# A 16-column bf16 product for one half of the array ahead of a stretch of unmasked attention scores

## The chip, the cores and the metric

The kernel runs on one core of a Trainium2 chip. The metric is the device time of one execution in microseconds, the median of three runs. Besides, one execution was taken by the hardware profiler; every row of a profile below is of that one execution.

## The reference

The model is two layers over eight batches of 512 tokens with 256 channels: a layer norm and attention (causal attention over the tokens plus cross attention to a context of 512 rows), a feed-forward block with quantised weights and activations, then cross attention to the same context and a second quantised feed-forward block. The change touches the attention scores of all three attentions, with 16 heads of 16 channels each:

```python
att  = jnp.einsum('bhqd,bhkd->bhqk', q, k) * scale
att  = jnp.where(causal[None, None], att, -jnp.inf)      # "S": causal
y    = jnp.einsum('bhqk,bhkd->bhqd', jax.nn.softmax(att, axis=-1), v)
attc = jnp.einsum('bhqd,bhkd->bhqk', qc, kc) * scale     # "C": to the context, no mask
y    = y + jnp.einsum('bhqk,bhkd->bhqd', jax.nn.softmax(attc, axis=-1), vc)
...
scores = jnp.einsum('bhqd,bhkd->bhqk', qh, kh) * scale   # "X": second layer, no mask
```

## The kernel before, in words

The attention work is cut into 24 units: eight causal ones (S), eight of the first layer's cross attention (C) and eight of the second layer's (X). A unit has four groups of four heads, and a group's scores are computed twice. First they are computed with queries on the partitions, into a pair of PSUM banks, only to find each row's maximum (`max_one`, L668; in the profile `pair<-qk`, read by VectorE as `mx<-pair`). Later they are computed with keys on the partitions, the maximum already subtracted through two extra rows, into two single banks, and ScalarE takes the exponential (`exp_one`, L756; in the profile `bank<-qk`, read by ScalarE as `p<-bank`). The exponentials are then multiplied with the values (`av_part`, `bank<-p,v`).

One call of `max_one` or `exp_one` is called a visit here. A visit handles two heads at once: head c=0 lies on partitions 0 to 63 and head c=1 on partitions 64 to 127, so that two products with a contraction over at most 64 rows use the two halves of the TensorE array side by side. In a C or X unit a visit is two f32 matmuls of 512 columns, one for each half, each with its own load of 128 weight columns. There are 8 max visits and 8 exp visits in a group, so 32 and 32 in a unit, and 512 and 512 in the 16 units of kind C and X.

In an S unit a visit begins with the mask: `masks` (L646) issues two small bf16 products (k = 0, 1) for each half that write minus 1e30 above the diagonal, and the f32 scores then add to them. In a C or X unit nothing stands ahead of the scores, and the first of them starts the bank anew (`start=off == 0 and kind != "S"`).

The order of all instructions on TensorE is fixed when the kernel is built. `Plan` holds clocks for the engines and estimates for each operation; the loop at L1452 picks, step by step, a max visit, an exp visit, a product with the values or a piece of another job (projections, transposes, feed-forward), and `plan.pe` moves TensorE's clock. The plan knows two ways of using the array that concern us: "rows" (two halves of 64 rows, all visits) and "cols" (four strips of 32 output columns, nearly all else), with a price for going from one to the other (`SWITCH`). So TensorE's stream is an alternation of stretches: some matmuls in columns, then one or several visits in a row, then columns again. A visit that follows matmuls of another kind is called a head below; one that follows another visit is called chained.

Which semaphores a visit waits for: the first matmul that writes a bank waits until VectorE (for a pair) or ScalarE (for a single bank) has read what stood there; `Writer.matmul` (L258) adds these waits to the first writer of a bank.

Of the kernel before, what the change touches and what calls it, by code (L numbers as in the profile page):

```python
# [76 lines left out]
class Plan:  # L77
# [39 lines left out]
    def op(self, kind, n, *deps):  # L117
        fixed, rate = RATE[kind]
        return self.run(kind.rstrip("2"), fixed + n * rate, *deps)
# [105 lines left out]
GQ, AHEAD = 4, 3  # L225
LINGER = 0.2
ROW_COLS = 600
DVE_HANDICAP = 0.8


# [56 lines left out]
def build(tc, A, out):  # L287
    nc = Engines(tc)
# [8 lines left out]
    plan = Plan()  # L297
# [3 lines left out]
    def tile(tag, shape, dtype, name, pool=wp):  # L301
        return pool.tile(shape, dtype, tag=tag, name=name, bufs=BUFS[tag])
# [52 lines left out]
    ident2 = const.tile([P, 2, P], BF16, name="ident2")  # L355
    mask2 = const.tile([P, 2, P], BF16, name="mask2")
# [29 lines left out]
    def evacuate(dst, src, n, *deps, bias=None):  # L386

        if plan.would("act", n, *deps) <= plan.would("dve", n, *deps) + DVE_HANDICAP:
            if bias is None:
# [256 lines left out]
    def masks(ps, c, blocks, keys):  # L646

        diag = ps.rearrange("p (a b) -> p a b", b=P)[:, blocks]  # L650
        rows = slice(64 * c, 64 * c + 64)
        for k in range(2):
            lhs, rhs = (mask2, ident2) if keys else (ident2, mask2)
            cols = slice(64 * k, 64 * k + 64 if keys else P)
            n = len(range(*blocks.indices(NT)))
            nc.tensor.matmul(
                diag[:, :, cols], lhs[rows, k], rhs[rows, k, cols].unsqueeze(1).broadcast_to([64, n, cols.stop - cols.start]),
                start=k == 0, stop=False, skip_group_check=True,
            )

    def max_ready(s):
        G, i = MAX_STEPS[s]
        t = plan.bank_at("sm")
        if ("stack", G) not in at or t is None or (i == 0 and G % 2 == 0 and not plan.rings["mx"]):
            return None
        return max(at["stack", G], t)

    def max_one(s):  # L668

        G, i = MAX_STEPS[s]  # L670
        kind, _ = UNITS[G // 4]
        p, qts = MAXS[kind][i]
        n = G // 2
        if i == 0 and G % 2 == 0:
            heapq.heappop(plan.rings["mx"])
            mx_t[n] = tile("mx", [P, 2, 4, NT], F32, f"mx{n}")
        pb = plan.bank_take("sm")
        ps = pairs[pb // 2]
        pair = 2 * (G % 2) + p
        size = [(qt + 1) * P if kind == "S" else T for qt in qts]  # L680
        offs = [sum(size[:x]) for x in range(len(qts))]
        if kind == "S":

            first = size[0] // P - 1
            step = size[-1] // P
            for c in range(2):
                masks(ps[:, c], c, slice(first, first + (len(qts) - 1) * step + 1, step), False)
            plan.pe(len(qts) * 192 + 60, mode="rows")
        for off, w, qt in zip(offs, size, qts):
            for c in range(2):  # L690
                q, k = (qk_t[n % NQK][64 * c : 64 * c + 48, pair, x] for x in range(2))
                nc.tensor.matmul(
                    ps[:, c, off : off + w], q[:, qt * P : (qt + 1) * P], k[:, :w],
                    start=off == 0 and kind != "S", stop=True, skip_group_check=True,
                )
        t = plan.pe(sum(size), mode="rows")
        for off, w, qt in zip(offs, size, qts):
            nc.vector.tensor_reduce(
                mx_t[n][:, :, pair, qt], ps[:, :, off : off + w], AX.X, ALU.max, negate=True
            )  # L700
            t = op("dve", 2 * w, t)
        plan.bank_give("sm", pb, t)
        if s + 1 == len(MAX_STEPS) or MAX_STEPS[s + 1][0] != G:
            at["max", G] = t

    def rows_job(n):
# [16 lines left out]
        for qt in range(NT):  # L723
            for h, i in enumerate(got):
# [4 lines left out]
                )  # L729
        tm = plan.pe(ROW_COLS, "rows")  # L730
        t = 0.0
# [24 lines left out]
    def exp_one(s):  # L756


        G, i = EXP_STEPS[s]
        kind, _ = UNITS[G // 4]  # L760
        p, kts = EXPS[kind][i]
        n = G // 2
        pair = 2 * (G % 2) + p
        pb = plan.bank_take("st", 2)
        tp, slots = zip(*(heapq.heappop(plan.p_free) for _ in range(2)))
        pt = [wp.tile([P, T], F32, tag=f"p{slots[c]}", name=f"p{G}_{i}_{c}", bufs=1) for c in range(2)]
        ps, off = [banks[x] for x in pb], 0
        if kind == "S":
            step = (T - kts[0] * P) // P
            for c in range(2):  # L770
                masks(ps[c], c, slice(0, (len(kts) - 1) * step + 1, step), True)
            plan.pe(len(kts) * P + 80, mode="rows")
        for kt in kts:
            q0 = kt * P if kind == "S" else 0
            w = T - q0
            for c in range(2):
                q, k = (qk_t[n % NQK][64 * c : 64 * c + 50, pair, x] for x in range(2))
                nc.tensor.matmul(
                    ps[c][:, off : off + w], k[:, kt * P : (kt + 1) * P], q[:, q0:],
                    start=off == 0 and kind != "S", stop=True, skip_group_check=True,  # L780
                )
                p_t[G, kt, 2 * p + c] = pt[c][:, off : off + w]
            off += w
        t = plan.pe(off, mode="rows")
        if s + 1 == len(EXP_STEPS) or EXP_STEPS[s + 1][0] != G:
            at["exp", G] = t
        tm = t
        for c in range(2):
            nc.scalar.activation(pt[c][:, :off], ps[c][:, :off], AF.Exp, scale=0.25)
            t = op("act", off, tm, tp[c])  # L790
            plan.bank_give("st", pb[c], t, c == 1)
        for kt in kts:
            p_at[G, kt, p] = t
        p_slots[G, kts[-1], p] = slots
# [657 lines left out]
    while plan.jobs or a < len(AV_STEPS):  # L1452
        ready = {
            "a": av_ready(a) if a < len(AV_STEPS) else None,
            "e": exp_ready(e) if e < len(EXP_STEPS) else None,
            "m": max_ready(m) if m < len(MAX_STEPS) else None,
        }
        can = {k: t is not None and t + LAT <= plan.now for k, t in ready.items()}
# [18 lines left out]
        if any(can.values()):  # L1477
            k = min(urgent)[1] if urgent else "e" if closing and can["e"] else "a" if can["a"] else min((feed[k], k) for k in "me" if can[k])[1]
            if k == "a":
                av_part(a)  # L1480
                a += 1
            elif k == "m":
                max_one(m)
                m += 1
            else:
                exp_one(e)
                e += 1
            idle = 0
        else:
            times = [t + LAT for t in ready.values() if t is not None] + [max(j[0], plan.now) for j in plan.jobs]  # L1490
            plan.clock["pe"] = max(before + 1e-3, min(times, default=before))
            idle += 1
            assert idle < 20000, (m, e, a)
# [100 lines left out]
    for bs in ((0,), (1,), (2, 3), (4, 5), (6, 7)):  # L1594
# [3 lines left out]
        for f in range(8):  # L1598
            i = 8 * b + n * f
            ps = [banks[2 + i % 6]] if n == 1 else [pairs[1 + f % 3][:, x] for x in range(2)]  # L1600
# [29 lines left out]
    def bias_first(i):  # L1630
        ps = half_banks[i % 8]
        nc.tensor.matmul(ps, ones3, b2p.rearrange("p t c -> p (t c)"), start=True, stop=False, skip_group_check=True)
        return ps.rearrange("p (t c) -> p t c", t=2)
# [53 lines left out]
    for i in range(2 * NB):  # L1687
# [4 lines left out]
        ps = half_ps.pop(i, None)  # L1692
        if ps is None:
            ps = bias_first(i)
# [79 lines left out]
```

## Time and profile before

| what | value |
|---|---|
| median of three runs | 1464.75 us (1461.56 to 1465.69) |
| the profiled execution, its own time | 1460.25 us |
| its span, first to last instruction | 1458.4 us |
| TensorE (PE) busy | 1374.8 us, 94%, 14400 matmuls and as many weight loads |
| VectorE (DVE) busy | 1142.0 us, 78% |
| ScalarE (ACT) busy | 1035.5 us, 71% |
| GpSimd (POOL) busy | 681.6 us, 47% |
| mean granted TensorE clock | 0.971 |

PE is the matmul side of TensorE, PEld its weight loads, which can overlap with matmuls. In the timeline a row gives the start, the length, the engine, the line, what is written and read, and how many instructions were merged; the end of a matmul is modelled, so that distances are best taken from start to start. A row such as `50*128 50x512 f32` is a product over 50 rows with 128 weight columns and 512 streamed columns.

### The profile page before, as it was taken

To read this page: it belongs to the slowest core of one execution; us is meant where nothing else is said; L and a number is where in the kernel's file an instruction comes from. 1 tells how busy PE (TensorE), PEld (TensorE's weight loads), DVE (VectorE), ACT (ScalarE), POOL (GpSimd) and SP (SyncE) were. 2 spreads that over 40 slices of the span, in tenths; PEclk is the share of its full clock that TensorE was granted. 3 is DMA by queue.
4 is the path that set the end of the run, shared out by engine and by line. 5 is a ranking of instruction groups with operands and counts; after the bars stand their busy time and mean duration, and the time that the engine had idled before them with its cause. 6 is when DMAs were issued, how large, how long until landed. Compare 5 with 4: busy or idle time off the path is not lost. (4 is left out here: it accounts for less than half of the span.)

```text
span 1458.4 us, 36089 instructions
## 1 busy us (share of the span) xinstructions
PE 1374.8 (94%) x14400; PEld 597.5 (41%) x14400; DVE 1142.0 (78%) x1591; ACT 1035.5 (71%) x1904; POOL 681.6 (47%) x1025
## 2 busy tenths in 40 slices
PE   4999999999999999999999999999999998999978
PEld 2443444444444444434344433443333333333527
DVE  4678588697788886898777996689899888766397
ACT  1456767677768867767677777668778795777587
POOL 1463355465455465464653552654455541524332
PEclk8899999999999999999899999999999999999899
DMA  6593565667576755665457655556647657373343
GB/s 126 152 216 76 133 139 125 142 138 182 132 161 150 161 129 141 156 161 126 105 126 155 163 126 132 142 120 160 163 105 169 155 149 196 105 176 110 117 142 116
DMA packets 155612, 207.03 MB, mean 142 GB/s; under 512 B 71940, under 2 KB 74244, under 8 KB 154932
## 3 DMA queue, kind: packets, MB, share of 16 engines
q1 hardware_dynamic: 155444, 204.73, 58.0%
q8 instruction: 113, 1.85, 0.5%
q14 instruction: 55, 0.45, 0.1%
HBM read 68.15 MB, written 47.43 MB: 79 GB/s over the span
## 5 line engine op out<-in xcount | busy, mean ns | idle before, releaser
L241 DVE TENSOR_REDUCE mx<-pair 128x2 f32<-128x1024 f32 (+3 forms) x768 | 808.9, 1086 | 210.7 <-PE pair L259 194.6
L241 ACT ACTIVATE p<-bank 128x512 f32<-128x512 f32 (+1 forms) x1408 | 712.0, 587 | 232.7 <-PE bank L259 224.8
L259 PE MATMUL bank<-p,v 128*32 128x512 f32 (+3 forms) x3072 | 371.7, 563 | 2.9 <-DVE mrow L241 1.3
L259 PE MATMUL bank<-qk 50*128 50x512 f32 (+3 forms) x1536 | 337.6, 433 | 16.2 <-ACT p L241 8.0
L259 PE MATMUL pair<-qk 48*128 48x512 f32 (+3 forms) x1536 | 325.5, 438 | 25.7 <-DVE mx L241 11.8
L259 PEld LDWEIGHTS bank<-qk 50*128 50x128 f32 x1536 | 159.6, 190 | 215.7 <-ACT p L241 142.9
L259 PEld LDWEIGHTS pair<-qk 48*128 48x128 f32 x1536 | 148.0, 191 | 171.5 <-DVE mx L241 83.4
L384 POOL TENSOR_SCALAR qkt<-qkt 128x512 fp32r<-128x512 f32 x92 | 57.1, 621 | 164.1 <-ACT qkt L241 157.5
L241 ACT ACTIVATE qkt<-bank,qk_bias 128x512 f32<-128x512 f32 x96 | 66.6, 693 | 81.0 <-PE bank L259 65.4
L409 POOL TENSOR_TENSOR qkt<-qkt 128x512 fp32r<-128x512 f32 x92 | 118.8, 1291 | 7.7
L259 PEld LDWEIGHTS bank<-p,v 128*32 128x32 f32 x3072 | 70.9, 109 | 114.6 <-issue 85.9
L384 POOL TENSOR_SCALAR mhl<-mx 128x32 fp32r<-128x32 f32 x48 | 11.8, 245 | 171.3 <-DVE mx L241 164.8
L883 POOL TENSOR_TENSOR yt<-oc,rb 128x512 f32<-128x512 f32 x31 | 39.8, 1283 | 73.3 <-DMA rb<-scrz 50.9
L259 PE MATMUL pair<-mask,ident 64*128 64x128 bf16 (+2 forms) x768 | 58.0, 226 | 6.9 <-DVE mx L241 4.7
L259 PE MATMUL bank<-ident,mask 64*128 64x64 bf16 (+1 forms) x768 | 52.7, 206 | 3.7 <-ACT p L241 1.2
L259 PEld LDWEIGHTS <-ident 64*128 64x128 bf16 x768 | 26.1, 97 | 71.0 <-issue 52.8
L259 PEld LDWEIGHTS <-mask 64*128 64x128 bf16 x768 | 25.8, 96 | 69.3 <-issue 61.0
L241 ACT COPY v<-bank 128x512 f32<-128x512 f32 x44 | 26.2, 596 | 39.4 <-PE bank L259 39.1
L241 ACT COPY ev<-bank 128x512 f32<-128x512 f32 x56 | 33.5, 598 | 17.9 <-PE bank L259 17.9
L241 DVE SCALAR_TENSOR_TENSOR h<-bank,so,bc_l_b 128x512 f32<-128x512 f32 x64 | 45.3, 741 | 0.9 <-PE bank L259 0.7
L241 ACT ACT_TABLE_LOAD x34 | 43.6, 1283 | 1.9 <-PEq L1762 0.7
L1189 POOL TENSOR_SCALAR h<-h,sh 128x1024 f32<-128x1024 f32 x32 | 36.0, 1125 | 17.7 <-DVE sh L241 15.2
(230 smaller groups left out, 1686.4 us busy)
## 6 DMA issues: line engine op xcount, KB each, us to landing
qk<-qkt SPq DMA_DIRECT2D x288, 256.0 KB
scro<-ev SPq DMA_DIRECT2D x94, 256.0 KB
oc<-scro SPq DMA_DIRECT2D x47, 256.0 KB
rb<-scrz SPq DMA_DIRECT2D x47, 256.0 KB
x_d<-xb SPq DMA_DIRECT2D x15, 512.0 KB
xa_s<-in_x SPq DMA_DIRECT2D x8, 512.0 KB
xb<-in_x SPq DMA_DIRECT2D x8, 512.0 KB
xr<-x_d SPq DMA_DIRECT2D x16, 256.0 KB
```

Of the source, the lines that this page charges most:

```text
L241: r = f(*args, **kw)
L259: r = self.eng.matmul(out, *args, **kw)
L384: nc.gpsimd.tensor_scalar(dst, src, 1.0, 0.0, ALU.mult, ALU.add)
L409: nc.gpsimd.tensor_tensor(dst, full, high.bitcast(F32), ALU.subtract)
L883: nc.gpsimd.tensor_tensor(y, o, rb, ALU.mult)
L1189: nc.gpsimd.tensor_scalar(ht, ht, s[:, t - t0 : t - t0 + 1], MAGIC, ALU.mult, ALU.add)
```

## The change

A new helper, `first_of_visit`, issues one bf16 matmul: its weights are `ident2[:64, 0]` (64 rows, 128 columns), the streamed operand is 16 columns of the mask (`NFIRST`), and the result goes to the first 16 columns of the c=0 half's score tile. Both visits call it in C and X units, at the place where an S visit has its masks, but it issues only if the plan's mode is not yet "rows": at a head, not in a chained visit. The scores that follow start the bank anew, so what it wrote is overwritten. Being the first writer of its bank, it takes over the wait for that bank. The plan's clock and mode are not moved by it, so the order of everything else stays.

```diff
+NFIRST = 16
...
+    def first_of_visit(ps):
+        if plan.mode != "rows":
+            nc.tensor.matmul(
+                ps[0][:, :NFIRST], ident2[:64, 0], mask2[:64, 0, :NFIRST], start=True, stop=True, skip_group_check=True
+            )
...
             plan.pe(len(qts) * 192 + 60, mode="rows")
+        else:
+            first_of_visit([ps[:, c] for c in range(2)])
         for off, w, qt in zip(offs, size, qts):
...
             plan.pe(len(kts) * P + 80, mode="rows")
+        else:
+            first_of_visit(ps)
         for kt in kts:
```

## The prediction

> **What bounds the kernel now.** I read the page first, then the groups by shape, then the timeline of TensorE in places where it did not wait, then the waits and the clock.
>
> ```profile
> PE 1374.8 (94%) x14400; PEld 597.5 (41%) x14400; DVE 1142.0 (78%) x1591; ACT 1035.5 (71%) x1904; POOL 681.6 (47%) x1025
> PE   4999999999999999999999999999999998999978
> PEclk8899999999999999999899999999999999999899
> ```
>
> TensorE is the busiest engine in nearly every slice; its matmuls are what the end waits for, though not at every moment:
>
> ```profile
> DVE mx L241 <- PE pair L259: 194.6, 239, 8.1
> PEld bank L259 <- ACT p L241: 157.8, 250, 2.6
> ```
>
> VectorE waited 194.6 us for max scores, and weight loads for exp scores waited 157.8 us for ScalarE to free a bank (part of that under running matmuls). So the engines take turns in holding each other up, and time added on TensorE counts in full only where it leads.
>
> The change adds a bf16 weight load and a 16-column matmul at the head of a stretch of visits. What a head costs now:
>
> ```profile
> L259 PEld LDWEIGHTS bank<-qk 50*128 50x128 f32 x1536 | 159.6, 190 | 215.7 <-ACT p L241 142.9 <-issue 34.4 <-DVE mx L241 10.0
> L259 PEld LDWEIGHTS <-mask 64*128 64x128 bf16 x768 | 25.8, 96 | 69.3 <-issue 61.0 <-DVE mx L241 3.0 <-DVE h L241 0.8
> ```
>
> An f32 load of scores lasts 190 ns, a bf16 load of the mask products 96. Next, TensorE's matmuls, start to start:
>
> ```profile
> 211.71 0.49 PE L259 MATMUL bank<-qk 50*128 50x512 f32 x2
> 212.14 0.42 PE L259 MATMUL bank<-p,v 128*32 128x128 f32 x8
> 212.49 0.49 PE L259 MATMUL bank<-qk 50*128 50x512 f32 x2
> 212.82 0.39 PE L259 MATMUL pair<-qk 48*128 48x512 f32 x2
> 213.15 0.64 PE L259 MATMUL bank<-xlt_s,w_Cq 128*32 128x512 f32 x4
> ```
>
> A lone visit (211.71 to 212.14) takes 0.43 us, 0.424 in the trace's finest numbers; a stretch of two (212.49 to 213.15) takes 0.66. The second visit costs only 0.23, because its weights came early:
>
> ```profile
> 1065.55 0.50 PE L259 MATMUL bank<-qk 50*128 50x512 f32 x2
> 1065.65 0.19 PEld L259 LDWEIGHTS pair<-qk 48*128 48x128 f32 x2
> 1065.88 0.40 PE L259 MATMUL pair<-qk 48*128 48x512 f32 x2
> 1066.21 0.64 PE L259 MATMUL bank<-p,v 128*32 128x512 f32 x4
> ```
>
> The second visit's load (1065.65) starts 0.23 us ahead of its matmul, under the first visit. The first visit's load has nothing to hide under: 0.10 us of each head is weights. A masked head has the change's pattern, bf16 ahead of f32:
>
> ```profile
> 68.16 0.24 PE L259 MATMUL bank<-ident,mask 64*128 64x64 bf16 x4
> 68.23 0.48 PE L259 MATMUL bank<-qk 50*128 50x512 f32 x2
> 68.64 0.27 PE L259 MATMUL bank<-l0w1s,one 128*128 128x1 f32 x1
> 68.16 0.12 PEld L259 LDWEIGHTS <-mask 64*128 64x128 bf16 x4 [0.20 <-issue]
> 68.20 0.20 PEld L259 LDWEIGHTS bank<-qk 50*128 50x128 f32 x2
> ```
>
> It takes 0.476 us to the next kind of work (68.16 to 68.64). The f32 load starts at 68.20 and the stretch ends 0.435 us after that; in the lone visit above it ends 0.424 after its load. Other masked heads agree (0.427 where a 64x128 mask stands ahead). So one rule covers heads: the end comes 0.425 to 0.435 us after the f32 weight load starts, whatever ran before it.
>
> **The change part by part.** It removes no work and moves none. It adds one load and one matmul per head. Chained visits get nothing, since the helper issues only when the mode is not "rows". Counted through the trace, 406 of the 1024 unmasked visits follow a matmul of another kind (222 exp, 184 max); 13 more follow the max rows' small transposes, where the mode is "rows" already. So 406 loads and 406 matmuls; TensorE goes from 14400 to 14806. No DMA, no VectorE, ScalarE or GpSimd instruction is added, and no queue is passed.
>
> Cost at one head: how much later does the f32 load of half c=0 start? In the masked heads, the second bf16 load starts 15 ns after the first one of the same half: a second weight set goes in as soon as the first product has its own. At a head of the changed kernel the f32 load is the second in that place, so it starts about 15 ns later than now; the end after it comes 0 to 10 ns later than the lone visit's (0.425 to 0.435 against 0.424). That gives 15 to 25 ns; I take 20. Streaming 16 columns (64 took 29 ns from the second mask product to the scores) runs under the f32 load. The c=1 half's load is not held up, but its matmul is issued behind that of c=0.
>
> Bounds: from above the masked exp head, which costs 0.476 - 0.424 = 52 ns with two bf16 products of 64 columns for each half; one product of 16 for one half can't well cost more. From below zero: the f32 load still has to come after the start of the stretch, and masked heads do not start sooner after the column work before them (0.525 us from its last matmul, 0.522 unmasked), so I see no gain at a head. Nearest row: 20 ns.
>
> The added instruction takes over the bank wait, so behind it stand the f32 load and all of TensorE's queue, as they stood behind the f32 load before; no wait is new. Where the head had waited, VectorE or ScalarE had just freed the bank and the 20 ns come after that.
>
> One rule of the Trainium skill speaks against the change: "TensorE: Matmul & The Clock Gate", Part 3 (The mechanism), says that a weight load runs beside matmuls in flight only if its row group differs. The f32 load of c=0 has the same rows as the small product, so it would wait for it, about 0.19 us (the shortest mask matmul), and 406 x 0.19 = 77 us would be lost. The trace disagrees: at 68.20 the f32 load runs while mask products of the same rows last to 68.40, and the load of 1065.65 runs under a matmul of the same rows. (Part 2 of the page, step 1, does allow a load into a background weight buffer ahead of matmuls in flight; that fits.) I follow the trace.
>
> Sum: 406 x 20 ns = 8.1 us on TensorE. How much reaches the end? Followed back from the last exp matmul, going at each wait to what ended it, TensorE holds 785 of 1347 us, and 213 of the 406 heads lie on that path: 213 x 20 ns = 4.3 us if the path stays. With more work TensorE leads more often; if always, 8.1. I take 6, against the profiled execution's 1460.25 (span 1458.4 and 1.85 around it): 1466.3. The three runs' median is 4.5 above that execution, so the prediction for a median is 1464.75 + 6 = 1470.8.
>
> **The rivals.** A difference of 0.3%, 4.4 us, is about what a measurement of this kernel can tell from no change.
>
> *Hidden.* The delays fall mostly where VectorE or ScalarE leads (VectorE is busy 51.60 of the 60 us from 1160 to 1220), and the next wait swallows them; or a head costs only 10 ns: 0 to 4 us, about 1467. For it: 193 heads off the path, waits everywhere. Against it: TensorE at 9 in nearly every slice. That the helper issues nothing (the mode is always "rows") would give 1464.75; but 406 heads follow column or full work, for which the plan sets another mode.
>
> *Faster, by the clock.* The granted clock falls to one half now and then:
>
> ```profile
> 703.00:710.00 7.00, 4.72 (x18) 1.63 (x18) 5.47 (x10) 2.74 (x5) 3.73 (x5) 0.68 0.40 93
> ```
>
> This is such a stretch, after a wait of 2 us (its columns: length, busy time of PE, PEld, DVE, ACT, POOL, then the clock, 0.68). Between 118 and 1245 us the clock record has seven stretches at half, 44 us together; a lone visit took 0.72 us there instead of 0.42, so they cost some 18 us. If the shifted stream waits less at one place, stretches vanish. To end below 1460.4 about 10.4 us must be won against the 6 lost, so over half of these stretches must go; three fifths gone gives 1459.5. For it: where they fall looks like chance. Against it: nothing in the change fills the long waits, and they may as well multiply.
>
> *Dearer heads.* The f32 load waits for more than the small load, and a head costs up to the masked head's 52 ns: 406 x 52 ns = 21 us, 16 to 21 at the end, about 1484. For it: the order of f32 behind bf16 for one half only is not in the trace. Against it: the 15 ns between loads of one half.
>
> **How the numbers follow.** Small cost as summed: 0.50, 1470.8, its own range 1468.5 to 1475. Hidden or nothing issued: 0.28. Faster by the clock: 0.12. Dearer: 0.10. So faster 0.12, same 0.28, slower 0.60. The range 1460 to 1482 holds the first two cases, the near end of the clock's and the low end of the dearer one.
>
> **What would show it.** 406 rows of a 64x16 bf16 product, and 14806 matmuls. A lone visit from 0.424 to about 0.44 to 0.45 us, start to start, with the f32 load 10 to 20 ns behind the bf16 one. A second visit still 0.23 to 0.235, its load still ahead. Waits of the weight loads for ScalarE and VectorE slightly smaller, VectorE's wait for scores slightly larger. Wrong if the lone visit shortens (then the weights do load under something), if it grows by 50 ns or more, or if the half-clock stretches between 118 and 1245 us differ from 44 us by more than 15.

## The result, and the profile after

The changed kernel took 1474.58 us, the median of six runs (1467.94 to 1480.08), against 1463.79 us before: ratio 1.0077, 95% interval 1.0053 to 1.0101. Forecast were 1470.8 us, a range of 1460 to 1482, and "slower" as the likeliest sign. In two later sets, on two chips, the same kernel gave 1.0061 (1.0039 to 1.0083) and 1.0071 (1.0046 to 1.0095). In all sets, runs more than 1.5% above the fastest of their kernel are left out as a slower state; this concerns two runs each of the kernels "f32 product" and "every visit" below.

The page of the changed kernel first, its busy times and the granted clock in 40 slices of the span (9 is 90% of full speed or more):

```profile
PE 1392.2 (94%) x14800; PEld 610.2 (41%) x14806; DVE 1141.0 (77%) x1591; ACT 1036.3 (70%) x1904; POOL 679.4 (46%) x1025
PEclk8799999999999999999999999999999998899899
```

The loads tell the count: 14806 against 14400, so 406 more, as counted (six matmul records are missing from this trace). All of them belong to C and X units; the causal S units are as they were. TensorE is 17.4 us busier, but this execution ran at a clock of 0.960 against 0.971; in the next profile of the changed kernel, at 0.969, TensorE is busy for 1382.7 us, 7.9 us more than before. The other engines are as before. The groups by shape show the new products and their loads (last columns: busy us and mean ns of one, then idle time and who ended it):

```profile
L260 PE MATMUL bank<-mask,ident 64*128 64x16 bf16 x222 | 40.0, 180 | 1.1 <-ACT p L242 1.1
L260 PE MATMUL pair<-mask,ident 64*128 64x16 bf16 x184 | 33.0, 180 | 1.7 <-DVE mx L242 1.6
L260 PEld LDWEIGHTS <-ident 64*128 64x128 bf16 x1174 | 64.3, 96 | 357.0 <-issue 311.0 <-ACT p L242 27.8 <-DVE mx L242 4.2
L260 PEld LDWEIGHTS bank<-qk 50*128 50x128 f32 x1536 | 163.7, 193 | 48.8 <-ACT p L242 26.7 <-DVE mx L242 7.2 <-issue 3.4
```

The rows count 222 heads of exp visits and 184 of max visits. Their busy time of 73 us overlaps with that of the scores that follow; it is not a cost. The same stretch of the program as was shown of before, in the timeline of TensorE's matmuls and then of its weight loads:

```profile
211.56 0.18 PE L260 MATMUL bank<-mask,ident 64*128 64x16 bf16 x1
211.56 0.51 PE L260 MATMUL bank<-qk 50*128 50x512 f32 x2
212.00 0.43 PE L260 MATMUL bank<-p,v 128*32 128x128 f32 x8
212.36 0.18 PE L260 MATMUL bank<-mask,ident 64*128 64x16 bf16 x1
212.37 0.51 PE L260 MATMUL bank<-qk 50*128 50x512 f32 x2
212.70 0.40 PE L260 MATMUL pair<-qk 48*128 48x512 f32 x2
213.03 1.05 PE L260 MATMUL bank<-xlt_s,w_Cq 128*32 128x512 f32 x6
...
211.55 0.09 PEld L260 LDWEIGHTS <-ident 64*128 64x128 bf16 x1 [0.41 <-issue]
211.56 0.20 PEld L260 LDWEIGHTS bank<-qk 50*128 50x128 f32 x2
...
212.51 0.19 PEld L260 LDWEIGHTS pair<-qk 48*128 48x128 f32 x2
```

The weight loads of the same lone visit before:

```profile
211.71 0.19 PEld L259 LDWEIGHTS bank<-qk 50*128 50x128 f32 x2 [0.41 <-issue]
```

The lone visit (211.56 to 212.00) takes 0.44 us where it took 0.43; the stretch of two (212.36 to 213.03) takes 0.67 where it took 0.66. The scores' f32 loads (211.56) start right behind the small bf16 load. The second visit's load (212.51) still comes early, 0.19 us ahead of its matmul.

Lone visits that did not wait fall into two close groups, near 424 and 432 ns before and near 440 and 447 after. The way from the last column matmul before into the stretch went from 522 to 525 ns. So a lone visit at the usual values costs 16 + 3 = 19 ns. Compared stretch by stretch over all heads that ran at full clock and did not wait in either trace, the cost is 15 ns on average (16 where one visit stands alone, 14 for two in a row, 13 for three), and the two later profiles of the changed kernel give 15 and 14 to 15. On TensorE that adds 406 x 15 ns = 6 us.

Taken apart in single loads, the cost is this. From the start of the last column matmul (f32, 512 columns), the later of the two f32 loads of a lone visit started at 524 ns, lasted 183 and ended at 707; now it starts at 527, lasts 197 and ends at 724 (medians). The two f32 matmuls, which started 3 ns apart, now start 35 ns apart.

The waits of the changed kernel (total us, times, longest):

```profile
PEld L260 <- issue: 405.9, 697, 2.0
ACT p L242 <- PE bank L260: 235.4, 279, 7.4
DVE mx L242 <- PE pair L260: 206.6, 248, 8.1
PEld bank L260 <- ACT p L242: 42.4, 112, 2.6
```

VectorE waits 12 us longer for scores than before, ScalarE 10.6 us longer (it had been 224.8). Part of that is this execution's low clock: in the two later profiles of the changed kernel, at 0.969, VectorE waits 201.9 and 200.7 us and ScalarE 230.2 and 229.0, against 194.6 and 224.8 of the first profile before and 198.7 and 227.0 of the second. So a few us of the added time pass through to the readers. That the f32 loads' wait for ScalarE fell from 157.8 to 42.4 is bookkeeping: at a head the wait now stands ahead of the small load, where the profile puts most of it down to "issue" (405.9 us, against 147.5 for bf16 loads before).

### The profile page after: what moved, and what is told of

It is laid out like the page before. It is cut to its first block, busy times and chain, and to the rows that moved or that the text cites. A ratio compares the mean times of both kernels' runs of the same rounds, so it can differ in the third digit from the quotient of the medians.

```text
span 1474.8 us, 36960 instructions
## 1 busy us (share of the span) xinstructions
PE 1392.2 (94%) x14800; PEld 610.2 (41%) x14806; DVE 1141.0 (77%) x1591; ACT 1036.3 (70%) x1904; POOL 679.4 (46%) x1025
## 5 line engine op out<-in xcount | busy, mean ns | idle before, releaser
L260 PE MATMUL bank<-qk 50*128 50x512 f32 (+3 forms) x1536 | 343.4, 433 | 15.4 <-ACT p L242 8.0
L260 PE MATMUL pair<-qk 48*128 48x512 f32 (+3 forms) x1536 | 329.9, 437 | 23.3 <-DMA qk<-qkt 10.7
L260 PEld LDWEIGHTS <-ident 64*128 64x128 bf16 x1174 | 64.3, 96 | 357.0 <-issue 311.0
L260 PEld LDWEIGHTS bank<-qk 50*128 50x128 f32 x1536 | 163.7, 193 | 48.8 <-ACT p L242 26.7
L260 PEld LDWEIGHTS pair<-qk 48*128 48x128 f32 x1536 | 151.8, 193 | 52.0 <-DVE mx L242 25.3
L260 PE MATMUL pair<-mask,ident 64*128 64x128 bf16 (+3 forms) x952 | 91.7, 218 | 8.6 <-DVE mx L242 6.3
L385 POOL TENSOR_SCALAR mhl<-mx 128x32 fp32r<-128x32 f32 x48 | 11.6, 242 | 171.9 <-DVE mx L242 165.6
```

Source lines behind the costliest of these rows:

```text
L260: r = self.eng.matmul(out, *args, **kw)
L385: nc.gpsimd.tensor_scalar(dst, src, 1.0, 0.0, ALU.mult, ALU.add)
```

## The experiments

Times are device microseconds. All runs but the first six of the kernel before have the mean granted clock beside them, and the time goes with it: one fit with a level for each kernel and a common slope gives 1.04 us less for each 0.001 of mean clock more. So each kernel is also given at equal clock, that is, as the fit has it when the clock is the same, with about twice the standard error. The kernel before has 101 runs in this fit, mean clock 0.9695.

| kernel | runs | ratio to before (95%) | mean clock | us over before at equal clock |
|---|---|---|---|---|
| changed, all three sets | 25 | 1.0077, 1.0061, 1.0071 | 0.9676 | 8.0 +- 1.0 |
| 128 columns, both sets | 35 | 1.0052, 1.0055 | 0.9693 | 7.2 +- 0.9 |
| both halves | 6 | 1.0083 (1.006 to 1.0105) | 0.9673 | 11.6 +- 1.9 |
| three products | 5 | 1.0165 (1.0139 to 1.0192) | 0.9682 | 20.7 +- 2.0 |
| f32 product | 4 | 1.0293 (1.0252 to 1.0335) | 0.9610 | 31.9 +- 2.4 |
| every visit | 4 | 1.0322 (1.0281 to 1.0363) | 0.9602 | 42.2 +- 2.4 |
| masks behind | 6 | 1.0086 (1.0058 to 1.0115) | 0.9682 | 9.0 +- 1.9 |
| masks ahead at heads only | 22 | 1.0013 (0.9996 to 1.0031) | 0.9679 | 0.1 +- 1.1 |

**The two kernels again, for their clock.** No edit; the changed kernel twice, on two chips.

> The kernel before, unchanged, for the granted clock of its runs. Theory one (heads: 406 stretches end some 18 ns later, 7.3 us; the rest of the difference is half-clock time that falls by chance): its mean clock over the runs lies within 0.003 of that of the changed kernel, 0.966, and its runs scatter between 0.96 and 0.972. Theory two (clock: the changed stream is granted half clock more often, systematically): it lies at 0.970 or above in nearly all runs, and at least 3 us of the difference is clock.

> The changed kernel again, beside the one before on the same chip. Theory one: 7 to 8 us slower at equal clock, ratio 1.004 to 1.007. Theory two: ratio 1.007 to 1.010, clock 0.964 to 0.967 against 0.970 or more.

> The changed kernel once more, for its clock. Theory one (the heads' 406 x 18 ns alone; the lower clock of its earlier runs was chance): mean clock 0.968 to 0.970, as before, and 7 to 8 us slower. Theory two (the emptier heads lower the granted clock): mean clock 0.967 or less, and 9 us or more slower.

The kernel before ran at 0.9987 of itself (0.9971 to 1.0003), mean clock 0.9697. That fits neither expectation for it: it is 0.0037 above 0.966, where theory one allowed 0.003, and half of its 14 runs lie under the 0.970 of theory two. The changed kernel had 0.9676 in the first of these sets and 0.9685 in the second, against 0.9690 and 0.9698 of before on the same chips. At equal clock 8.0 us are lost, which is theory one's 7 to 8. Over all sets the changed kernel's clock is 0.0019 lower, worth 2 us, and these make up the rest of its 10 us. Theory two's clock of 0.967 or less did not come in these two sets, though its 9 us or more did in the second (9.45 us between the medians); theory one's 0.968 or more came in the second set only. Whether the change itself lowers the clock a little is open. The profiled executions alone would mislead: the first one of the changed kernel had 61 us of half clock between 118 and 1330 us where before had 44, but the next had 51, and before, taken again, 55.

**Both halves.**

```diff
-            nc.tensor.matmul(
-                ps[0][:, :NFIRST], ident2[:64, 0], mask2[:64, 0, :NFIRST], ...
+            for c in range(2):
+                rows = slice(64 * c, 64 * c + 64)
+                nc.tensor.matmul(
+                    ps[c][:, :NFIRST], ident2[rows, 0], mask2[rows, 0, :NFIRST], ...
```

> The changed kernel with the small product for both halves of the array, so 812 products in place of 406. Theory one (what counts is how late the f32 weight load of a half starts, and both halves load side by side): a lone visit stays within 440 to 450 ns from start to start, and the time within 3 us of the changed kernel. The rival (each small product costs its own issue and stream on TensorE): twice the cost, a lone visit near 455 to 460 ns and 7 us more than the changed kernel.

A lone visit takes 443 or 450 ns, about as theory one said, and a head costs 18 ns on average where it cost 15; twice the products did not cost twice. The time is 3.6 us over the changed kernel at equal clock, a little more than theory one's 3 and, with an error of 2 us, less clearly under the rival's 7. For the end, then, half the array or all of it makes little difference.

**Every visit.**

```diff
-        if plan.mode != "rows":
-            nc.tensor.matmul(...)
+        nc.tensor.matmul(...)
```

> The small product in every one of the 1024 unmasked visits, chained ones too. Theory one (the f32 load of a chained visit can't come ahead of the small product): a chained visit grows by about 100 ns where its load was hidden; summed over the trace 45.4 us for the loads that came early and 18 us for the rest, 64 us on TensorE, of which at least 26 us reach the end; expected 35 to 60 us slower than before, ratio 1.024 to 1.041. The rival (only the switch to rows makes the small product dear): 1024 x 18 ns = 18 us at most, ratio 1.013 or less.

The timeline of a stretch of two max visits in this kernel, matmuls and then weight loads:

```profile
88.59 0.18 PE L260 MATMUL pair<-mask,ident 64*128 64x16 bf16 x1
88.60 0.51 PE L260 MATMUL pair<-qk 48*128 48x512 f32 x2
88.99 0.17 PE L260 MATMUL pair<-mask,ident 64*128 64x16 bf16 x1
89.00 0.50 PE L260 MATMUL pair<-qk 48*128 48x512 f32 x2
89.42 0.64 PE L260 MATMUL bank<-p,v 128*32 128x512 f32 x4
...
88.95 0.09 PEld L260 LDWEIGHTS <-ident 64*128 64x128 bf16 x1 [0.16 <-issue]
88.99 0.19 PEld L260 LDWEIGHTS pair<-qk 48*128 48x128 f32 x2
```

The bf16 load (88.95) now stands ahead of the f32 load, which comes at 88.99, together with the small product and no longer some 0.2 us ahead of the scores. A chained visit that ends its stretch takes some 445 ns at the median where it took some 330. At equal clock 42.2 us are lost, inside theory one's 35 to 60 and over twice the rival's 18. The condition in the helper is what keeps the change small. The clock fell as well, to 0.9602 on average.

**Three products.**

```diff
-            nc.tensor.matmul(...)
+            for _ in range(3):
+                nc.tensor.matmul(...)
```

> Three small bf16 products in a row at each of the 406 heads, in place of one. Theory one (the scores' f32 load can start only when the last small product has started): products start some 39 and 29 ns after one another, so the f32 load starts about 70 ns later than with one, a lone visit takes 500 to 510 ns, and 406 x 85 ns = 34 us are lost against the kernel before at equal clock, 30 to 38 with the clock. The rival (a head's cost is a fixed price of going from f32 or bf16 columns to rows by way of a bf16 load): a lone visit stays at 440 to 460 ns, and the loss at 8 to 15 us.

A lone visit in this kernel, matmuls:

```profile
212.09 0.18 PE L260 MATMUL bank<-mask,ident 64*128 64x16 bf16 x1
212.10 0.50 PE L260 MATMUL bank<-qk 50*128 50x512 f32 x1
212.13 0.19 PE L260 MATMUL bank<-mask,ident 64*128 64x16 bf16 x2
212.18 0.48 PE L260 MATMUL bank<-qk 50*128 50x512 f32 x1
212.59 0.32 PE L260 MATMUL bank<-p,v 128*32 128x128 f32 x4
```

It takes 0.49 us, a little under the 0.50 to 0.51 expected; the products follow each other by 39 and 25 ns, and one of the two f32 products of scores (212.18) comes behind all three. The rival's 440 to 460 ns is out. Stretch by stretch a head costs 57 ns more than before on average, so 406 x 57 ns = 23 us were added on TensorE; 20.7 us are lost at equal clock. That is under theory one's 34 and above the rival's 8 to 15.

**An f32 product.**

```diff
-                ps[0][:, :NFIRST], ident2[:64, 0], mask2[:64, 0, :NFIRST], ...
+                ps[0][:, :NFIRST], ident_r[:64], ident_r[:64, :NFIRST], ...
```

> The small product at a head with f32 weights and f32 columns (the identity) in place of bf16. Theory one (a bf16 load delays its product by some 10 ns, an f32 load by some 98): the small product waits 98 ns for its weights, the scores' f32 load starts only then, a lone visit takes 525 to 540 ns, and 406 x 105 ns = 43 us are lost. The rival (any small product costs the same, the type doesn't matter): 7 to 11 us.

A head in this kernel, matmuls and then weight loads:

```profile
312.49 0.27 PE L260 MATMUL pair<-ident_r 64*128 64x16 f32 x1
312.49 0.60 PE L260 MATMUL pair<-qk 48*128 48x512 f32 x2
313.02 0.64 PE L260 MATMUL bank<-xlt_s,w_Sk 128*32 128x512 f32 x4
...
312.49 0.18 PEld L260 LDWEIGHTS pair<-ident_r 64*128 64x128 f32 x1 [0.84 <-DVE mx L242]
312.49 0.29 PEld L260 LDWEIGHTS pair<-qk 48*128 48x128 f32 x2
```

A lone visit takes 533 or 540 ns, some 108 more than before: two f32 loads one after the other, as theory one said. So the price of such a product is that of its weights. Stretch by stretch a head costs 104 ns more on average, 406 x 104 ns = 42 us; at equal clock 31.9 us are lost, about three quarters, and with the lower clock 43, which is theory one's figure.

**128 columns.**

```diff
-NFIRST = 16
+NFIRST = 128
```

> The small product with 128 streamed columns in place of 16, nothing else. Theory one (its stream runs under the f32 load of the scores, which takes about 98 ns): 128 columns, some 55 ns, are hidden, a lone visit stays within 5 ns of 440, and the time within 3 us of the changed kernel. The rival (streaming adds to the head): 47 ns more for each head, a lone visit near 487 ns, 19 us more than the changed kernel.

> The changed kernel with 128 streamed columns in place of 16, once more, beside the changed kernel on the same chip. Theory one: the same time and clock as the changed kernel, within 2 us. Theory two (the 16-column product leaves the array emptier than the 128-column one): its clock is above that of the changed kernel by 0.002 or more, and it is 2 to 3 us faster.

A lone visit in this kernel:

```profile
209.95 0.23 PE L260 MATMUL bank<-mask,ident 64*128 64x128 bf16 x1
209.96 0.51 PE L260 MATMUL bank<-qk 50*128 50x512 f32 x2
210.39 0.42 PE L260 MATMUL bank<-p,v 128*32 128x256 f32 x4
```

It is still 0.44 us, with eight times the columns: the stream runs under the f32 load, and the rival's 19 us over the changed kernel did not appear (7.2 us over before at equal clock, where the changed kernel has 8.0). Against the changed kernel on the same chip the clock was 0.9689 to 0.9685, not 0.002 higher, and the time 1.7 us lower on average; theory two for this pair is not borne out.

**Masks behind the scores.** Of the kernel before, with no small product. The first change is in `masks`, the others in `max_one` and likewise in `exp_one`:

```diff
-                start=k == 0, stop=False, skip_group_check=True,
+                start=False, stop=k == 1, skip_group_check=True,
...
-            for c in range(2):
-                masks(ps[:, c], c, ..., False)
-            plan.pe(len(qts) * 192 + 60, mode="rows")
         for off, w, qt in zip(offs, size, qts):
...
-                    start=off == 0 and kind != "S", stop=True, skip_group_check=True,
+                    start=off == 0, stop=kind != "S", skip_group_check=True,
...
         t = plan.pe(sum(size), mode="rows")
+        if kind == "S":
+            for c in range(2):
+                masks(ps[:, c], c, ..., False)
+            t = plan.pe(len(qts) * 192 + 60, mode="rows")
```

> The kernel before, with the mask products of the S visits behind the scores in place of ahead of them; no small product. Theory one (a bf16 product ahead of f32 scores keeps the f32 load from coming early): in the 249 masked visits that are chained the f32 load is hidden again, 75 to 100 ns each, 19 to 25 us on TensorE, while masked heads stay as they are; expected 8 to 22 us faster than before, ratio 0.985 to 0.995. The rival (the masks' place does not matter to the loads): within 3 us of before.

This expectation failed: 9.0 us slower at equal clock. A masked max visit with an exp visit behind it shows why, in the timeline of this kernel:

```profile
259.27 0.39 PE L259 MATMUL pair<-qk 48*128 48x256 f32 x2
259.50 0.26 PE L259 MATMUL pair<-mask,ident 64*128 64x128 bf16 x4
259.59 0.48 PE L259 MATMUL bank<-qk 50*128 50x512 f32 x2
260.00 0.32 PE L259 MATMUL bank<-ident_r,xa_s 128*32 128x128 f32 x4
...
259.56 0.19 PEld L259 LDWEIGHTS bank<-qk 50*128 50x128 f32 x2
```

The stretch of the same make-up before:

```profile
253.25 0.26 PE L259 MATMUL pair<-mask,ident 64*128 64x128 bf16 x4
253.35 0.37 PE L259 MATMUL pair<-qk 48*128 48x256 f32 x2
253.55 0.41 PE L259 MATMUL bank<-qk 50*128 50x512 f32 x2
253.88 0.32 PE L259 MATMUL bank<-ident_r,xa_s 128*32 128x128 f32 x4
...
253.43 0.19 PEld L259 LDWEIGHTS bank<-qk 50*128 50x128 f32 x2
```

The next visit's f32 load (259.56) comes only with the second mask product, 0.03 us ahead of its matmul where it had come 0.12 us ahead (253.43), and this stretch takes 0.735 us where its like before took 0.631. The cost was passed on to the next visit, not saved. At a masked head that stands alone it even grew, from 476 to 502 ns and, for another shape, from 508 to 561. That the masks had run under the f32 load there, and now follow the scores, is the likely reason; it was not tested. Only a masked visit that is chained and ends its stretch got shorter (some 70 ns).

**Masks ahead at heads, behind in chained visits.** The last kernel with a condition, so that only the visits that can gain are turned:

```diff
+        ahead = kind == "S" and plan.mode != "rows"
+        if ahead:
+            mask()
...
+        if kind == "S" and not ahead:
+            t = mask()
```

> The kernel before with the masks of an S visit ahead of its scores at a head, and behind them in a chained visit; no small product. Theory one (a bf16 product ahead of f32 scores hinders the early f32 load only where there was one to hinder): heads stay at 476 and 502 ns, a chained masked visit that ends its stretch gets 70 ns shorter, 116 times, 8 us on TensorE, and one in the middle passes its cost on to the next visit; 3 to 8 us faster than before at equal clock, ratio 0.994 to 0.998. The rival (masks behind the scores cost something beyond the loads): 3 us or more slower, as with all masks behind.

A chained masked visit that ends its stretch, in this kernel:

```profile
224.71 0.50 PE L259 MATMUL bank<-qk 50*128 50x512 f32 x2
225.05 0.28 PE L259 MATMUL pair<-qk 48*128 48x256 f32 x2
225.17 0.26 PE L259 MATMUL pair<-mask,ident 64*128 64x128 bf16 x4
225.36 0.64 PE L259 MATMUL bank<-p,v 128*32 128x512 f32 x4
```

The stretch of this make-up before:

```profile
225.65 0.49 PE L259 MATMUL bank<-qk 50*128 50x512 f32 x2
225.98 0.26 PE L259 MATMUL pair<-mask,ident 64*128 64x128 bf16 x4
226.08 0.36 PE L259 MATMUL pair<-qk 48*128 48x256 f32 x2
226.37 0.64 PE L259 MATMUL bank<-p,v 128*32 128x512 f32 x4
```

It takes 0.65 us from 224.71 to 225.36; before, it took 0.72 (225.65 to 226.37). So the local gain of 70 ns is there, but the time did not move: 0.1 +- 1.1 us at equal clock, ratio 1.0013 (0.9996 to 1.0031). Over the masked stretches that ran at full clock in both traces, only 0.9 us came off: those that end in a masked chained visit got 3.6 us shorter where nothing waited and 1.9 us longer where something did, and the others got 0.8 us longer. Both the expected gain and the rival's loss are refuted; the expected 8 us were not there even in the masked stretches. No version beat the kernel before.

## Why the prediction was right or wrong

*The count of heads* was right: 406, with 222 and 184.

*The cost of a head*, 15 to 25 ns with 20 taken, held: 19 ns at a lone visit's usual values, 15 on average. Its division did not. The f32 load was to start 15 ns later and the end to come up to 10 ns after that; it starts only 3 ns later than the later load did before, and 14 ns of the cost are in the load itself, which lasts 197 ns instead of 183. The expected sign that the f32 load stands 10 to 20 ns behind the bf16 one did not come either: it is 6 to 7 ns. What the prediction rested on, that the end of a head follows the f32 load, is borne out in a sharper form, by the load's end: at lone visits the later f32 load ends at 707 ns before (counted as above), at 724 with the change and with 128 columns, at 728 with both halves, at 774 with three products and at 815 with the f32 product, and in each of these kernels the next column work starts 241 to 247 ns after that end (medians).

*How much reaches the end* was mis-sized. Of 8.1 us the prediction let 6 arrive, between the 4.3 of the old path and all of it. At equal clock 8.0 +- 1.0 us arrived, and the heads added 6 (at 15 ns) to 7.7 (at 19): all of it, and perhaps a little more, whose place is not known. The path followed back through the old trace, with 213 of 406 heads on it, was a lower bound and no more. A cost taken a little high and a share taken too low offset each other in part, and that is luck. Of the larger additions of the same kind some nine tenths (three products) and three quarters (the f32 product) arrived at equal clock.

*The clock* was brought in as a rival that could make the kernel faster. It went the other way, if anywhere: 0.0019 lower on average, 2 us, though not by as much on each chip. In the first set, where the medians differ by 10.8 us and not by the 6 forecast, the changed kernel's mean clock was 0.9657, its lowest. The prediction named half-clock time between 118 and 1245 us that differs from 44 us by more than 15 as a sign of error. It did not occur: the first profile of the changed kernel has 44.5 us there. Just behind that window it has 17 us more than before, which the repeated profiles put within the scatter. In two other kernels the clock is clearly lower (0.960 with the product in every visit, 0.961 with the f32 product), which goes with some 9 to 10 us in each.

*The rule* quoted in the prediction from the Trainium skill, that a load runs beside matmuls in flight only if its row group differs, would have cost 77 us; 10 came. The trace was the better guide.

*The dearer heads* (52 ns) and the *hidden* case did not come about. Of the other expected signs, the second visit's early load and VectorE's longer wait came as said; the f32 loads' smaller wait is there, but only because it is now counted with another load.

## What to carry to other kernels

In this kernel a small product ahead of a large one on TensorE cost what it did to the large one's weight load: 15 to 19 ns where that load was bare anyway and the small one's weights were bf16, and some 0.11 us where the load had been coming early or where the small one's weights were f32. Look at the start and the end of the load against its matmul before putting anything between. And a few nanoseconds added at each of 406 places on the busiest engine arrived in full, while 70 ns saved at some stretches did not show in the time: a gain has to be summed over all stretches, those that wait too, before it is counted.

## What the runs showed of the hardware that was not expected

The two halves of the array did not keep the program's order between them. In the kernel with three products the order of issue is three small products for c=0, then the scores of c=0, then those of c=1. The rows of it above show one f32 matmul at 212.10, ahead of the second and third small product at 212.13, and the other at 212.18. A row does not name its half; that the early one is c=1, which needs no weights of c=0, is the natural reading. With the one-half product the two f32 matmuls of a lone visit start 35 ns apart, and their weight loads end 15 ns apart.

The granted clock was lower in two kernels in which TensorE was hardly ever idle for long: 0.961 where each of 406 heads took 0.1 us more (the f32 product) and 0.960 with a small product in every visit, against 0.9695 before. It is not simply the length of the stalls: three products, with 0.06 us more at the same 406 heads, had 0.9682. What lowers it stays open.
